# A third tile of rows, and longer waits between the stages of a chunk's tail

## Chip, cores and metric

The kernel runs on one core of one Trainium2 chip. The metric is device microseconds of one execution; times given for the kernel are medians over several runs.

## What is computed

One layer of graph attention on x (8 frames, 2048 rows, 256 channels) with a 2048 x 2048 adjacency mask, all in float32. Cut to what matters:

```python
qkv = x @ w_qkv                                   # 8 heads of 32 channels
scores = q @ k.T / sqrt(32), masked to -1e9 where adj == 0
t = softmax(scores) @ v
y = layernorm(x + t) * g1 + be1
f = relu(y @ w1 + b1) @ w2 + b2
z = layernorm(y + f) * g2 + be2
out = layernorm(x + z)
```

## The kernel before

**Main loop.** The 1024 items of `fast_path` are (frame f, chunk qc of 512 query rows, head group g of four heads, block mb of 128 keys): 8 x 4 x 2 x 16. An item is one step t of the loop at L599. In it, TensorE makes the scores of item t + 2 (`scores`, L222 to L234) in pairs of PSUM banks; VectorE adds the mask to them and writes an SBUF tile `p` of 128 x 2048 (L233, two instructions); ScalarE takes the exponential of item t + 1 in place (L237); TensorE multiplies item t's `p` with the values (L249) into the group's bank. The pool `pp` has 12 tiles. A chunk is two groups of 16 steps, so 32 steps.

**Sums of p.** The softmax denominators are column sums of all 16 `p` tiles. `add_up` folds them into few: blocks 3, 6, 8, 11, 13, 15 are added to block 0 by POOL (L271); two chains of three are added into blocks 1 and 2 by accumulating DMAs that POOL issues (L268); block 14 stays alone. `denominator` then multiplies the four tiles that remain with ones (L315), the last of them, block 0, not before `advance` has reached the step `ready`, which is the group's last step plus `SUM`. The sum is copied out of PSUM into `dT` (L317), transposed (L95) and inverted (L326).

**Side work.** Everything else is written as Python generators in the list `fill`: x transposes (`turn`), projections (`project`, `ask`), denominators, and, for each chunk, `outcome` (divides the attention result, adds x by an accumulating DMA, L339) and `tail`. `advance(t)` runs at the head of each step and resumes those that are ready, sorted by a due step. A number that a generator yields is a wait of so many steps; BANK asks for a PSUM bank, one new one per step; MORE asks to go on with the bank; WAIT holds it; ROOM waits until fewer than the allowed number of tails is open; TURNED waits for the tiles of the feed-forward part. Each step has credit for about one piece of matmul work, and for more only when something is due. All this is fixed when the program is built: on the chip each engine runs its instructions in that order and waits on semaphores.

**Tail of a chunk.** `tail` works on a tile `y` from the pool `yp` (two tiles): `norm` (statistics on VectorE, L278 and L279; 1 / sigma and the bias `nb` on POOL, L283 to L287; scale and shift on ScalarE, L290), `feed_forward` (transposes, rows g1r and be1b2r on POOL at L459 and L461, first products with `w1s`, second with `w2s`, sum at L483), `norm`, rows g2r and be2r on POOL (L363, L365), x added by DMA (L367), `norm`, and the store (L370). `per` is how many of the four row blocks are done in one step. In the last frame the chunk before the last uses `per` 2; the last chunk goes through `finish`, in two halves.

**Masks.** The mask of a chunk is 8 tiles of fp8, each for two blocks; they are made once, kept in DRAM, and loaded by SP for each later chunk (L151), into a pool `mkp` of 9 tiles. SP also issues the x and xT loads, the xT stores and the output.

Of the kernel before, what the change touches and what calls it, by code (L numbers as in the profile page):

```python
# [19 lines left out]
P = 128  # L20
# [41 lines left out]
def fast_path(ctx, tc, cst, x, adj, out, RS):  # L62
# [6 lines left out]
    mkp = ctx.enter_context(tc.tile_pool(name="mkp", bufs=MB // 2 + 1))  # L69
# [6 lines left out]
    yp = ctx.enter_context(tc.tile_pool(name="yp", bufs=2))  # L76
# [185 lines left out]
    SUM = 4  # L262
# [11 lines left out]
    def norm(t, per=1):  # L274
        mv = small.tile([P, TPC, nc.vector.BN_AGGR_DIM], F32, name="mv")
        for j in range(TPC):
            st = small.tile([P, nc.vector.BN_STATS_DIM], F32, name="st")
            nc.vector.bn_stats(st, t[:, j, :])  # L278
            nc.vector.bn_aggr(mv[:, j, :], st)  # L279
            if j % per == per - 1:  # L280
                yield 1
        rs = small.tile([P, TPC], F32, name="rs")
        nc.gpsimd.tensor_scalar(rs, mv[:, :, 1], EPS, 1.0, op0=ALU.add, op1=ALU.mult)  # L283
        nc.gpsimd.tensor_tensor(rs, rs, cst["mhalf"], ALU.pow)  # L284
        nb = small.tile([P, TPC], F32, name="nb")
        nc.gpsimd.tensor_tensor(nb, mv[:, :, 0], rs, ALU.mult)
        nc.gpsimd.tensor_scalar(nb, nb, -1.0, 1.0, op0=ALU.mult, op1=ALU.mult)  # L287
        yield 2
        for j in range(TPC):
            nc.scalar.activation(t[:, j, :], t[:, j, :], AF.Identity, bias=nb[:, j:j + 1], scale=rs[:, j:j + 1])  # L290
            if j % per == per - 1:
                yield 1
# [4 lines left out]
    def denominator(f, qc, g, ready):  # L297
# [7 lines left out]
        ps = bank()  # L305
        for n, block in enumerate(blocks):
# [4 lines left out]
            term = PT.pop((f, qc, g, block))  # L311
            state["credit"] -= 4 * CH
# [3 lines left out]
        dT = op.tile([P, CH], F32, name="dT")  # L316
# [16 lines left out]
    def outcome(f, qc):  # L333
# [7 lines left out]
        if (f, qc) == (F - 1, NCK - 2):  # L341
            start(begin + 5, tail(f, qc, y, xin, 2), begin + 8)
        else:
            start(begin + 10, tail(f, qc, y, xin), begin + 26)
# [12 lines left out]
    def tail(f, qc, y, xin, per=1):  # L357
# [10 lines left out]
        yield 7  # L368
# [68 lines left out]
    def finish(f, qc):  # L437
# [6 lines left out]
        while both:  # L444
            for e in list(both):
                if next(e, both) is both:
                    both.remove(e)

    def feed_forward(y):
# [22 lines left out]
        yield 1  # L472
# [31 lines left out]
    def advance(t, finish=False):  # L504
# [15 lines left out]
        for e in list(fill):  # L520
            while e[2] is not None and e[0] <= t and e is not state["holder"]:
# [8 lines left out]
                elif e[2] == TURNED and state["turned"] or e[2] == ROOM and state["tails"] == 2:  # L530
# [6 lines left out]
    LEAD = 2  # L537
# [61 lines left out]
    for t, (f, qc, g, mb) in enumerate(items):  # L599
        if g == 1 and mb % 2 and (f + 1 < F or qc + 1 < NCK):  # L600
            load_mask(f + (qc + 1) // NCK, (qc + 1) % NCK, mb // 2)
# [269 lines left out]
```

## Time and profile before

| what | value |
|---|---|
| median of 3 runs | 3241.72 us (3237.86 to 3245.61) |
| the profiled execution, own time | 3246.02 us |
| its span, first to last instruction | 3244.1 us |
| mean granted TensorE clock | 0.985 |
| TensorE matmuls busy | 3109.4 us, 96% |
| VectorE, ScalarE, POOL busy | 84%, 75%, 80% |
| L233 mask additions on VectorE | 2409.3 us, mean 1218 ns |
| L237 exponentials on ScalarE | 1956.1 us, mean 1910 ns |
| L271 sums on POOL | 1825.5 us, mean 4793 ns |
| mask loads by SP | 248, 128 KB each |

The profile is of one execution. A wait is put down to what ended it. "Busy" of TensorE is modelled from the instructions' sizes; engines wait in order, so an engine's idle time costs only where the work that ends last stands behind it. Times in the timeline count from the start of the span.

### The profile page before, as it was taken

To read this page: it belongs to the slowest core of one execution; us is meant where nothing else is said; L and a number is where in the kernel's file an instruction comes from. 1 tells how busy PE (TensorE), PEld (TensorE's weight loads), DVE (VectorE), ACT (ScalarE), POOL (GpSimd) and SP (SyncE) were. 2 spreads that over 40 slices of the span, in tenths; PEclk is the share of its full clock that TensorE was granted. 3 is DMA by queue.
4 is the path that set the end of the run, shared out by engine and by line. 5 is a ranking of instruction groups with operands and counts; after the bars stand their busy time and mean duration, and the time that the engine had idled before them with its cause. 6 is when DMAs were issued, how large, how long until landed. Compare 5 with 4: busy or idle time off the path is not lost.

```text
span 3244.1 us, 68406 instructions
## 1 busy us (share of the span) xinstructions
PE 3109.4 (96%) x28996; PEld 979.0 (30%) x28996; DVE 2735.7 (84%) x3203; ACT 2435.8 (75%) x1941; POOL 2592.2 (80%) x1358
## 2 busy tenths in 40 slices
PE   7899999999999999999999999999999999998985
PEld 4222333223332233322233323323233323332222
DVE  4888888888888888888988888888888888888975
ACT  3667778777777777778777778777778777777774
POOL 0568888888878888788887888888888788878884
PEclk8899999999999999999999999999999999999998
DMA  9688779778879788788787879878788878877763
GB/s 320 145 181 185 183 176 199 178 177 196 181 176 207 171 188 193 159 195 200 178 181 174 185 174 221 177 167 198 173 192 197 177 168 198 181 171 161 166 145 86
DMA packets 153240, 590.52 MB, mean 182 GB/s; under 512 B 15040, under 2 KB 67776, under 8 KB 103904
## 3 DMA queue, kind: packets, MB, share of 16 engines
q0 software_dynamic: 64416, 434.80, 66.9%
q1 hardware_dynamic: 87696, 149.98, 13.1%
q8 instruction: 229, 3.75, 0.4%
q10 hardware_dynamic: 816, 1.31, 0.1%
q14 instruction: 83, 0.68, 0.1%
HBM read 146.67 MB, written 37.75 MB: 57 GB/s over the span
## 4 chain that ended last, share of the span: by engine, by line
PE 75%; DVE 7%; POOL 5%; issue 4%; DMA 4%; ACT 2%; DVEq 0%; POOLq 0%; ACTq 0%
PE s L230 27%; PE x L249 24%; PE x L54 14%; PE x L315 6%; DVE p L233 6%; PE x L95 4%; DMA p<-p 3%; POOL p L271 2%; ACT p L237 1%; DMA mask<-md 1%; POOL y L365 1%; DVE st L278 1%; POOL y L363 0%; POOL y L461 0%; POOL y L459 0%
## 5 line engine op out<-in xcount | busy, mean ns | idle before, releaser
L233 DVE TENSOR_TENSOR p<-s,mask 128x1024 f32<-128x1024 f32 x2048 | 2409.3, 1218 | 372.7 <-PE s L230 209.9
L237 ACT ACTIVATE p<-p 128x2048 f32<-128x2048 f32 x1024 | 1956.1, 1910 | 521.4 <-DVE p L233 465.6
L271 POOL TENSOR_TENSOR p<-p 128x2048 f32<-128x2048 f32 x381 | 1825.5, 4793 | 223.7 <-ACT p L237 221.3
L230 PE MATMUL s<-qT,kT 32*128 32x512 f32 x8192 | 1173.8, 643 | 40.8 <-DVE p L233 35.9
L249 PE MATMUL x<-p,v 128*32 128x512 f32 x8192 | 1096.0, 607 | 16.7 <-ACT p L237 16.4
L268 POOL DMA_DIRECT2D p<-p x383 | 359.3, 956 | 306.9 <-ACT p L237 88.3
L230 PEld LDWEIGHTS s<-qT,kT 32*128 32x128 f32 x8192 | 321.1, 183 | 644.7 <-DVE p L233 587.2
L249 PEld LDWEIGHTS x<-p,v 128*32 128x32 f32 x8192 | 161.6, 108 | 797.8 <-issue 310.6
L315 PE MATMUL x<-p,ones 128*32 128x512 f32 x2080 | 268.2, 594 | 17.9 <-POOL p L271 11.1
L290 ACT ACTIVATE y<-y,nb,rs 128x256 f32<-128x256 f32 x372 | 218.7, 590 | 40.4 <-POOL nb L287 40.4
L54 PE MATMUL x<-in,wqkv 128*32 128x512 f32 x1888 | 243.5, 592 | 0.0
L278 DVE BATCH_NORM_STATS2 st<-y 128x6 f32<-128x256 f32 x372 | 154.9, 416 | 5.1 <-DMA y<-in_x_dram 5.1
L54 PE MATMUL x<-turned,w1s 128*32 128x512 f32 x992 | 123.5, 596 | 0.4 <-ACT in L166 0.4
L54 PE MATMUL x<-w2s,hT 128*32 128x256 f32 x2016 | 121.8, 382 | 2.1 <-DVE y L483 2.1
L54 PEld LDWEIGHTS x<-wqkv,in 128*32 128x32 f32 x3584 | 102.2, 110 | 63.4 <-issue 58.9
L315 PEld LDWEIGHTS x<-p,ones 128*32 128x32 f32 x2080 | 66.3, 110 | 178.2 <-issue 140.4
L54 PE MATMUL x<-wqkv,in 128*32 128x128 f32 x3584 | 117.3, 273 | 0.0
L54 PEld LDWEIGHTS x<-in,wqkv 128*32 128x32 f32 x1888 | 61.7, 110 | 140.9 <-issue 113.7
L284 POOL TENSOR_TENSOR rs<-rs,mhalf 128x4 f32<-128x4 f32 x93 | 96.3, 1036 | 7.8
L54 PEld LDWEIGHTS x<-w2s,hT 128*32 128x32 f32 x2016 | 65.4, 111 | 75.0 <-issue 33.0
L363 POOL TENSOR_TENSOR y<-y,g2r 128x1024 f32<-128x1024 f32 x31 | 82.5, 2663 | 5.3 <-ACT y L290 5.3
L461 POOL TENSOR_TENSOR y<-y,be1b2r 128x1024 f32<-128x1024 f32 x31 | 83.0, 2679 | 0.6
(116 smaller groups left out, 1335.7 us busy)
## 6 DMA issues: line engine op xcount, KB each, us to landing
p<-p POOLq DMA_DIRECT2D x383, 1024.0 KB, 10.4
in<-xd SPq DMA_DIRECT2D x87, 512.0 KB, 10.6
mask<-md SPq DMA_DIRECT2D x248, 128.0 KB, 7.9
y<-in_x_dram POOLq DMA_DIRECT2D x62, 512.0 KB, 8.1
p<-in_adj_dram SPq DMA_DIRECT2D x16, 1024.0 KB, 10.7
out_dram<-y SPq DMA_DIRECT2D x31, 512.0 KB, 6.2
in<-in_x_dram SPq DMA_DIRECT2D x29, 512.0 KB, 15.5
xd<-in SPq DMA_DIRECT2D x28, 512.0 KB, 11.2
```

The source lines that it names most:

```text
L54: nc.tensor.matmul(out[r:r + D], lhsT[:, r:r + D], rhs, start=start, stop=stop)
L95: nc.tensor.transpose(ps[:, j * P:(j + 1) * P], s, ident)
L230: nc.tensor.matmul(ps2[half][:, j, :], KT[f, mb // TPC, g][r:r + D, (mb % TPC) * P:(mb % TPC + 1) * P], QT[f, qc, g][r:r + D, :], start=Tr ...
L233: nc.vector.tensor_tensor(pt[:, 2 * half:2 * half + 2, :], ps, MK[f, qc, mb // 2][:, mb % 2, None, :].to_broadcast([P, 2, CH]), ALU.add)
L237: nc.scalar.activation(PT[item], PT[item], AF.Exp, scale=1.0 / math.sqrt(D))
L249: nc.tensor.matmul(O[grp][r:r + D, :], V[f, mb // TPC, g][:, mb % TPC, r:r + D], PT[item][:, h, :], start=(mb == 0), stop=(mb == LAST))
L268: nc.gpsimd.dma_start(PT[f, qc, g, chain[0]], PT.pop(item), accum_op=ALU.add)
L271: nc.gpsimd.tensor_tensor(first, first, PT.pop(item), ALU.add)
L278: nc.vector.bn_stats(st, t[:, j, :])
L284: nc.gpsimd.tensor_tensor(rs, rs, cst["mhalf"], ALU.pow)
L290: nc.scalar.activation(t[:, j, :], t[:, j, :], AF.Identity, bias=nb[:, j:j + 1], scale=rs[:, j:j + 1])
L315: nc.tensor.matmul(ps[r:r + D, :], cst["ones"], term[:, h, :], start=(n == 0), stop=(n == len(blocks) - 1))
```

## The change

The pool of row tiles `yp` goes from 2 to 3, and up to three tails may be open. The room for it comes from the mask pool (9 to 8 tiles) and from the tile `dT`, which is dropped: the copied denominators go into the first quarter of the first term's `p` tile. Mask loads are written six steps later in the program (`LATE`). `SUM` goes from 4 to 5. `norm` waits 4 steps (3 with `per` 2) and not 2 between POOL's part and ScalarE's; the second products wait 3 steps and not 1; the last norm waits 9 (7 with `per` 2) and not 7. Tails start 12 steps after their division and not 10, with a later due step; in the last frame all tails use `per` 2 and start 8 steps after it (before, only that of the chunk before the last, 5 steps after it). `finish` gives way for a step after each round of its two halves.

```diff
--- before.py
+++ after.py
@@ -66,14 +66,14 @@
 
     LD = 3
     dp = ctx.enter_context(tc.tile_pool(name="dp", bufs=1, space=bass.MemoryType.DRAM))
-    mkp = ctx.enter_context(tc.tile_pool(name="mkp", bufs=MB // 2 + 1))
+    mkp = ctx.enter_context(tc.tile_pool(name="mkp", bufs=MB // 2))
     ld = ctx.enter_context(tc.tile_pool(name="ld", bufs=LD))
     kp = ctx.enter_context(tc.tile_pool(name="kp", bufs=3 * NCK - 1))
     qp = ctx.enter_context(tc.tile_pool(name="qp", bufs=4))
     vp = ctx.enter_context(tc.tile_pool(name="vp", bufs=3 * NCK - 1))
     pp = ctx.enter_context(tc.tile_pool(name="pp", bufs=12))
     work = ctx.enter_context(tc.tile_pool(name="work", bufs=1))
-    yp = ctx.enter_context(tc.tile_pool(name="yp", bufs=2))
+    yp = ctx.enter_context(tc.tile_pool(name="yp", bufs=3))
     op = ctx.enter_context(tc.tile_pool(name="op", bufs=1))
     small = ctx.enter_context(tc.tile_pool(name="small", bufs=4))
 
@@ -259,7 +259,7 @@
     ALONE = 14
 
     ENDED = MB - 5
-    SUM = 4
+    SUM = 5
 
     def add_up(item):
         f, qc, g, mb = item
@@ -285,7 +285,7 @@
         nb = small.tile([P, TPC], F32, name="nb")
         nc.gpsimd.tensor_tensor(nb, mv[:, :, 0], rs, ALU.mult)
         nc.gpsimd.tensor_scalar(nb, nb, -1.0, 1.0, op0=ALU.mult, op1=ALU.mult)
-        yield 2
+        yield max(5 - per, 2)
         for j in range(TPC):
             nc.scalar.activation(t[:, j, :], t[:, j, :], AF.Identity, bias=nb[:, j:j + 1], scale=rs[:, j:j + 1])
             if j % per == per - 1:
@@ -303,17 +303,19 @@
             late = {n: len(items) - k for n, k in ((2, 2), (3, 1), (4, 1), (5, 0), (6, 0), (7, 0))}
         yield BANK
         ps = bank()
+        spare = None
         for n, block in enumerate(blocks):
             if n:
                 yield MORE
             while state["now"] < late.get(n, 0):
                 yield WAIT
             term = PT.pop((f, qc, g, block))
+            spare = spare or term
             state["credit"] -= 4 * CH
             for h in range(4):
                 r = D * h
                 nc.tensor.matmul(ps[r:r + D, :], cst["ones"], term[:, h, :], start=(n == 0), stop=(n == len(blocks) - 1))
-        dT = op.tile([P, CH], F32, name="dT")
+        dT = spare[:, 0, :]
         nc.scalar.copy(dT, ps)
         yield 1
         yield BANK
@@ -338,10 +340,10 @@
         yield from divide(f, qc, y)
         nc.gpsimd.dma_start(y, xin, accum_op=ALU.add)
         begin = items.index((f, qc, 1, LAST)) + SUM + 2
-        if (f, qc) == (F - 1, NCK - 2):
-            start(begin + 5, tail(f, qc, y, xin, 2), begin + 8)
+        if f == F - 1:
+            start(begin + 8, tail(f, qc, y, xin, 2), begin + 12)
         else:
-            start(begin + 10, tail(f, qc, y, xin), begin + 26)
+            start(begin + 12, tail(f, qc, y, xin), begin + 30)
 
     def divide(f, qc, y):
         rc = RC.pop((f, qc))
@@ -365,7 +367,7 @@
         nc.gpsimd.tensor_tensor(z, z, rows(cst["be2r"]), ALU.add)
         yield 1
         nc.gpsimd.dma_start(z, xin, accum_op=ALU.add)
-        yield 7
+        yield 11 - 2 * per
         yield from norm(z, per)
         nc.sync.dma_start(out[f, qc * CH:(qc + 1) * CH, :].rearrange("(p j) c -> p j c", p=P), z)
         state["tails"] -= 1
@@ -445,6 +447,7 @@
             for e in list(both):
                 if next(e, both) is both:
                     both.remove(e)
+            yield 1
 
     def feed_forward(y):
         yield TURNED
@@ -469,7 +472,7 @@
                 columns(ps, w1s[:, a, d * P:(d + 1) * P], yT[:, a, :], start=(a == 0), stop=(a == 1))
             nc.scalar.activation(hT[:, d, :], ps, AF.Relu, bias=cst["b1s"][:, d:d + 1], scale=1.0)
         state["turned"] = False
-        yield 1
+        yield 3
         z = y
         for jj in range(0, TPC, 2):
             yield BANK
@@ -527,14 +530,14 @@
                     inputs = inputs and not any(u is not None for u in live[:INPUTS - e[2]])
                     if not inputs:
                         break
-                elif e[2] == TURNED and state["turned"] or e[2] == ROOM and state["tails"] == 2:
+                elif e[2] == TURNED and state["turned"] or e[2] == ROOM and state["tails"] == 3:
                     break
                 resume(e, t)
             while e is state["holder"] and more():
                 resume(e, t)
 
     items = [(f, qc, g, mb) for f in range(F) for qc in range(NCK) for g in range(2) for mb in range(MB)]
-    LEAD = 2
+    LEAD, LATE = 2, 6
     FRAME = 2 * NCK * MB
 
 
@@ -597,8 +600,9 @@
         pass
     state["side"] = 0
     for t, (f, qc, g, mb) in enumerate(items):
-        if g == 1 and mb % 2 and (f + 1 < F or qc + 1 < NCK):
-            load_mask(f + (qc + 1) // NCK, (qc + 1) % NCK, mb // 2)
+        uf, uqc, ug, umb = items[max(t - LATE, 0)]
+        if ug == 1 and umb % 2 and (uf + 1 < F or uqc + 1 < NCK):
+            load_mask(uf + (uqc + 1) // NCK, (uqc + 1) % NCK, umb // 2)
         for what, *which in NEXT.get(t % FRAME, []):
             to = f if what is ask and which[0] else f + 1
             if to < F:
```

## The prediction

> **What bounds the kernel now.** I read the page's busy shares first, then PE's own waits, then the timeline around one of its gaps.
>
> ```profile
> PE 3109.4 (96%) x28996; PEld 979.0 (30%) x28996; DVE 2735.7 (84%) x3203; ACT 2435.8 (75%) x1941; POOL 2592.2 (80%) x1358
> ```
>
> PE is the bound, but its busy time is modelled, so I checked it by steps. In the timeline the gap from the first L249 matmul of one step to that of the next depends only on the side work ("fill") between them. I call eight L54 or L315 matmuls (32 small ones for V or the second products), or four transposes, a unit. Medians: one unit 2.92 us, two 3.78, transposes of dT or oT 2.75, of y 2.65, nothing 2.56 (2.49 at best). A unit is thus 3.78 - 2.92 = 0.86, a step without fill would need 2.06, and an **empty step** wastes about 0.45: there DVE's two L233 adds (2.36) set the pace. A steady frame of 128 steps holds 144 units, 18 of them second in their step, and 2 empty steps (144 - 18 + 2 = 128).
>
> What a step takes beyond its kind's median is a stall. Frames 1 to 6: 41.0 us in all. Frame 7: 20.9. Frame 0: 8.6. The waits of PE name the releasers:
>
> ```profile
> PE s L230 <- DVE p L233: 35.9, 64, 6.5
> PE x L249 <- ACT p L237: 16.4, 10, 5.1
> ...
> PE x L315 <- POOL p L271: 11.1, 6, 2.1
> ...
> PE x L315 <- DMA p<-p: 6.9, 5, 3.9
> ```
>
> Columns: total us, times, longest. The third is a denominator term waiting for POOL's sums, the second a value product waiting for the exponential. Why the exponential is late shows in the timeline of frame 3, group 3 (groups of 16 steps, numbered from 0), step 14:
>
> ```profile
> 1427.85 4.88 POOL L271 TENSOR_TENSOR p<-p 128x2048 f32<-128x2048 f32 x1
> ...
> 1434.50 0.19 POOL L287 TENSOR_SCALAR nb<-nb 128x4 f32<-128x4 f32 x1
> ...
> 1434.73 0.60 ACT L290 ACTIVATE y<-y,nb,rs 128x256 f32<-128x256 f32 x1 [4.05 <-POOL nb L287]
> ...
> 1435.23 1.89 ACT L237 ACTIVATE p<-p 128x2048 f32<-128x2048 f32 x1
> ...
> 1437.18 0.64 PE L249 MATMUL x<-p,v 128*32 128x512 f32 x4 [2.19 <-ACT p L237]
> ```
>
> The norm's small POOL operations queue behind a 4.88 us addition; ACT reaches the norm two steps after they were issued, sits 4.05 us, the exponential behind it starts late, and PE idles 2.19 us. The same spot costs in every frame from 1 on.
>
> **What the Trainium skill says.** "Perfetto Trace Analysis", section Per-engine timelines, says that ACT, DVE and GPSIMD take work strictly first in, first out: the three lines from nb to L237 agree. The same page, section Optimization Strategy, advises finding the saturated engine's gaps and what releases them; repeating gaps may mean missing buffers. Here the repeated gap is a late POOL result; no row shows DVE waiting for a y buffer. "GPSIMD Engine Reference", section Elementwise — side-by-side cycle accounting, gives 4497 ns for a 2048-element fp32 addition; L271's mean here is 4793, so POOL spends 1.6 steps on each of six such sums per 16 steps, and lag of two steps is easy.
>
> **The change part by part.** Steps r count from the first step after a 512-row chunk ends; a chunk has 32.
>
> *Norms wait 4 steps instead of 2 (3 with two rows at a time).* No instruction is added. Two steps are 5.8 us, more than the 4.05. Group 3 steps 14 and 15, frames 1 to 6: 1.42, 1.69, 2.26, 1.91, 0.90, 1.97, 1.70 = 11.9; group 7 step 11: 1.20 and 0.35. Of 13.4 I take 12 off. In frame 7 the same stall is 5.13 + 1.40; only one step is gained, but the older tail also runs at other steps: 4.5 off, of 6.5. Between zero and all is the bound.
>
> *SUM 4 to 5.* The fourth term was held to `advance` 19 after its group began and would be held to 20. I looked at where it falls: counting the fill after step s as s, it comes at 3 or later in 62 of 63 groups (19 times at 3, which is `advance` 20), once at 2. So the hold itself binds once, at most one empty step, 0.45: I take zero. Its other effect is that division starts at 6 and not 5, behind dT at the same place: zero, at most one step.
>
> *Tail start +2, product wait 1 to 3, last norm 2 later.* These move POOL's four 2.6 us row operations. Before, L363 and L365 fall between step 12 of even groups and step 1 of odd ones, where additions 13 and 15 of the sum chain also queue. In frame 3 they ran at 1484.32 and 1491.16, addition 15 from 1494.75 to 1499.63, and the fourth term waited: group 5 steps 2 to 4 cost 2.56, 3.86, 1.59, 3.86, 1.81, 3.60 = 17.3, group 7 step 3 another 0.8. After, by hand: norm 18 to 29, y transposed at 30 and 31, first products 33 to 36, denominators next, second products about 39 to 41, norm to 53, L363 at 54 and 55, step 6 or 7 of odd groups, far from the closing sums. L459 and L461 come at 0 or 1 of even groups, behind addition 15, as they already do in group 2 without a stall. I take 11 of 18.1, because third terms also wait for the DMA sums, whose issues share POOL; bound 0 to 18. The second products' own wait (group 6 step 0, on L461 through L483) is 0.73 + 1.14 + 0.41 + 0.65 = 2.9: two more steps, all off.
>
> *Last frame.* All three tails now start at +8. The third-last DVE stop is the clearest gain:
>
> ```profile
> 3118.78 0.87 POOL L339 DMA_DIRECT2D y<-in_x_dram  x1 [1.47 <-DVE y L353]
> ...
> 3128.36 0.43 DVE L278 BATCH_NORM_STATS2 st<-y 128x6 f32<-128x256 f32 x1 [5.13 <-DMA y<-in_x_dram]
> ...
> 3130.80 2.09 PE L230 MATMUL s<-qT,kT 32*128 32x512 f32 x8 [6.52 <-DVE p L233]
> ```
>
> The statistics are issued two steps after the transfer, which takes 9.5 us; DVE's mask additions queue behind. Steps 10 and 11 of group 6 lose 7.10 + 1.22. With three to four more steps the transfer has landed: 8 off. At the end, the last chunk no longer runs as one block; the second-last tail's L363 and L365 (2.40 each) stand on POOL ahead of the finish's first norm, about 3 us late, while its four statistics (2.3) go between the finish's and not behind: +2 net, -3 to +5.
>
> *Longer tails, third y tile.* A tail lasts from step 6 to about 77 where it was 5 to some 66 (counted from the code's yields and the steps above); two per 64 steps no longer suffice, the third removes a wait of the next chunk at ROOM. Covered: 0; without it each chunk would slip some ten steps.
>
> *dT in the first term's tile.* No copy is added; L317 writes another place. The tile stays until the transposes, 3 to 7 steps longer. Unfinished p tiles peak at 10 of 12 when a group begins (4 old heads, 3 new, 3 in the pipeline), and the kept tile is one of the four: 0, at worst a DVE wait of under a step (2 us) per group.
>
> *Masks: 8 tiles, loaded 6 steps later.* The 248 loads and SP's issue cost stay. Before, a mask landed 41 us (median; least 20.7) before the L233 that reads it, and took 10.1 us to land (longest 23.4). One tile fewer frees it two steps later, -6; on SP it now queues behind six more steps of x and xT transfers and out stores, each of which may wait for ACT. If SP keeps step exactly it is issued 6.5 steps, 19 us, ahead. Mostly covered; 1 us for a few late ones, 20 at the bound. The x and xT loads no longer stand behind masks that wait for their tile: nothing PE shows, 0.
>
> *Fill.* The product phase leaves the end of odd groups. There steps 9 to 15 may lack units, though projections move up. I allow 2 more empty steps per frame, 7 x 2 x 0.45 = 6; bounds -6 (the present 2 go) and +20.
>
> **Sum.** 12 + 4.5 + 11 + 2.9 + 8 = 38.4 off; 2 + 1 + 6 on, and 2 for POOL lag meeting a wait elsewhere: -27. The profiled execution took 3246.0 (span 3244.1 and 1.9 around it), 4.3 above the median; it becomes 3219, the median 3241.7 - 27 = **3215**.
>
> **Rivals.**
> - *POOL's lag only moves.* POOL is 80% busy either way; the denominators' 17.3 stay and the norms' stall reappears at other steps: only 2.9 + 8 + 6 off against 11 on: about 3236. For it: the hold of SUM doesn't bind. Against: group 2 has this phase now, and no stall.
> - *SUM alone does nothing and the rest works:* that is inside my sum already, the group 5 loss then stays wholly: 3226.
> - *Slower: empty steps.* Each tail moves five units out of odd groups. If projections can't fill them (an xT needs a free `in` tile), 31 chunks x 5 x 0.45 = 70 us come on against 38: 3241.7 + 32 = 3274. It decides from 38 / 31 / 0.45 = 2.7 more empty steps per chunk. Against it: 14 units of projections and x transposes per chunk have only about 12 free steps, so backlog should fill them; group 1 shows such backlog as double steps.
>
> **How the numbers follow.** Main course 0.57, SUM rival 0.13, lag moves 0.15, slower 0.15 (empty steps, with late masks in it). About 0.2%, 6.5 us, is what a measurement here tells from no change. The first two lie below 3235; of the third 0.02 does, and 0.13 lies within: faster 0.72, same 0.13, slower 0.15. Range: all stalls gone and no new empty step gives 3195; the top takes in the milder slower cases, 3252.
>
> **What would show it.** Right: L290 waits for nb fall from 40.4 us to under 10; the 6.52 us gap is gone; L363 runs in steps 5 to 8 of odd groups; L315 waits for POOL are halved; 2 to 5 empty steps per frame. Wrong: over 8 empty steps per frame, DVE waits on mask loads, or L315's waits at a new step.

## The result, and the profile after

The kernel after takes **3381.99 us** (median of 4 runs, 3377.37 to 3382.84) against 3242.98 (median of 4) for the kernel before: a ratio of 1.0428, 95% interval 1.041 to 1.0446. It is 139 us slower; the forecast was 27 us faster, with a range that ended at 3252. The profiled execution is the run of 3377.37, its span 3375.5 us: 131.4 more than before.

Busy times, from the page's first part:

```profile
PE 3143.5 (93%) x28996; PEld 982.2 (29%) x28996; DVE 2736.5 (81%) x3203; ACT 2440.3 (72%) x1941; POOL 2590.3 (77%) x1358
```

No engine has more to do: the instruction counts are those of before, and DVE and POOL are busy within 2 us of before. PE's modelled busy time is 34 us up, its share down from 96 to 93%. So the 131 us are waits. The granted clock is no rival: it was 0.985 before and 0.980 after, and the median of a step with one unit is 2.92 us in both. The waits of the kernel after (total us, times, longest), DVE's lines first, then PE's:

```profile
DVE p L233 <- PE s L230: 209.3, 333, 6.0
DVE p L233 <- DMA p<-p: 164.7, 67, 6.3
```

```profile
PE s L230 <- DVE p L233: 147.5, 180, 3.9
...
PE x L317 <- DMA p<-p: 6.0, 3, 3.4
...
PE x L249 <- ACT p L237: 2.8, 5, 1.3
```

The same DVE line of the kernel before:

```profile
DVE p L233 <- DMA p<-p: 1.7, 1, 1.7
```

The line to see is the second. DVE's mask addition L233 writes a fresh `p` tile, and that tile was last read by a sum made by DMA. Before, it waited for such a sum once, for 1.7 us; now 67 times, 164.7 us. PE then waits for DVE's scores (35.9 us before, 147.5 now). PE's waits for a term from POOL (11.1 before) are gone from the list, and those for the exponential fell from 16.4 to 2.8: what the forecast aimed at did go. (Lines move by two or three: L315, L353, L363, L365, L459 and L461 of before are L317, L355, L365, L367, L462 and L464 after.)

The step method of the prediction says where. Each entry is the time that steps took beyond the median that their kind has in the kernel before, an empty step with the 0.5 us or so that it wastes; "even" and "odd" are groups of 16 steps, numbered from 0 in a frame, with step numbers within the group:

| kernel | even 0-3 | even 4-10 | even 11-15 | odd 0-6 | odd 7-13 | odd 14-15 | frames 0 and 7 | all | span |
|---|---|---|---|---|---|---|---|---|---|
| before | 3.3 | 3.9 | 6.3 | 19.3 | 3.8 | 12.0 | 49.4 | 98.0 | 3244.1 |
| after | 22.8 | 68.4 | 28.7 | 0.6 | 28.4 | 0.2 | 79.8 | 228.7 | 3375.5 |

The first six columns are frames 1 to 6. The totals differ by 130.7, the spans by 131.4: the table holds the whole loss. The old stalls (odd 0-6, odd 14-15) are gone, and four new ones stand elsewhere.

**Where it comes from.** The largest, even 4 to 10, in frame 3, group 4. POOL before, from just ahead of the group (which starts at 1440.96):

```profile
1437.58 2.69 POOL L461 TENSOR_TENSOR y<-y,be1b2r 128x1024 f32<-128x1024 f32 x1
1439.92 14.10 POOL L271 TENSOR_TENSOR p<-p 128x2048 f32<-128x2048 f32 x3
1453.93 0.88 POOL L268 DMA_DIRECT2D p<-p  x1
```

And after (the group starts at 1499.57, its step 7 at 1521.98):

```profile
1499.81 9.52 POOL L271 TENSOR_TENSOR p<-p 128x2048 f32<-128x2048 f32 x2
1509.28 2.38 POOL L462 TENSOR_TENSOR y<-y,g1r 128x1024 f32<-128x1024 f32 x1
1511.75 2.38 POOL L464 TENSOR_TENSOR y<-y,be1b2r 128x1024 f32<-128x1024 f32 x1
1514.08 4.59 POOL L271 TENSOR_TENSOR p<-p 128x2048 f32<-128x2048 f32 x1
1518.58 0.88 POOL L268 DMA_DIRECT2D p<-p  x1
```

Before, the row operation was over when the group began: three sums, then the DMA that adds block 4 (L268), 13.0 us into the group. Now L462 and L464 stand between the second and the third of those sums, and the DMA is issued 19.0 us into it. From its issue to its landing it takes 7.0 us (median), and until then block 4's tile is not free. Here is DVE, which needs that tile for the scores of step 7:

```profile
1518.70 2.36 DVE L233 TENSOR_TENSOR p<-s,mask 128x1024 f32<-128x1024 f32 x2 [0.86 <-POOL p L271]
1526.23 2.35 DVE L233 TENSOR_TENSOR p<-s,mask 128x1024 f32<-128x1024 f32 x2 [5.18 <-DMA p<-p]
...
1532.05 2.35 DVE L233 TENSOR_TENSOR p<-s,mask 128x1024 f32<-128x1024 f32 x2 [2.87 <-DMA p<-p]
```

The transfer lands at 1526.11, DVE goes on at 1526.23, and steps 7 and 8 are 3.1 and 1.8 us too long. The second wait, at 1532.05, ends with the sum of block 5, the next that POOL issued. Followed landing by landing, DVE's 164.7 us are 82.9 for block 4, 53.9 for block 5, and 27.3 for blocks 10 and 12 of the group before.

The late sum also meets fewer free tiles. In this group four steps of first products now go ahead of the denominators. Before, the four remaining `p` tiles of the ended group were let go one by one at steps 2 to 5; now three go at steps 5 and 6, and the one that lends its first quarter to `dT` at step 9, with the transposes. With so few free tiles, DVE meets the one that a transfer still reads. How much a late sum would cost with the tiles let go early, no run shows by itself. "Perfetto Trace Analysis", section Optimization Strategy, says that the same gap repeating on the engine that should be saturated can mean too little memory for the next tile. In the kernel before no line showed that; in this one the 67 waits do. "DMA: Bandwidth & Descriptors", section Anatomy of one DMA — SWDGE (gpsimd) path, puts any semaphore wait of a transfer on the issuing engine; the tail experiments below show that on POOL.

The stall at even 0-3 is the same wait, with the last sums of the odd group before it. POOL in frame 5, group 3, and then DVE in step 1 of group 4:

```profile
2290.71 2.37 POOL L367 TENSOR_TENSOR y<-y,be2r 128x1024 f32<-128x1024 f32 x1
2293.02 0.91 POOL L268 DMA_DIRECT2D p<-p  x1
```

```profile
2317.46 2.36 DVE L233 TENSOR_TENSOR p<-s,mask 128x1024 f32<-128x1024 f32 x2 [2.30 <-DMA p<-p]
```

L365 and L367 now start at steps 5 and 8 of odd groups, and L367 stands ahead of the DMA of block 7, which goes out at step 8.96 (median) where it was 7.64. Block 10 follows it in the same chain and lands 3.6 us after the even group has begun, where it was 0.7 us ahead of it. In these steps of frames 1 to 6 DVE waits 23.0 us for the sums of blocks 10 and 12.

The even 11-15 stall is of another kind, in frame 3, group 4 again:

```profile
1540.24 0.42 DVE L278 BATCH_NORM_STATS2 st<-y 128x6 f32<-128x256 f32 x1
1540.70 0.18 DVE L279 BATCH_NORM_AGGREGATE mv<-st 128x2 f32<-128x6 f32 x1
1540.80 0.66 DVE L355 TENSOR_TENSOR y<-x,rc 128x512 f32<-128x512 f32 x1
1541.37 2.35 DVE L233 TENSOR_TENSOR p<-s,mask 128x1024 f32<-128x1024 f32 x2
```

The second norm's statistics and the next chunk's division L355 fall in the same two steps. DVE needs from 1540.24 to 1543.63, 3.39 us, in steps that PE's transposes would end in 2.75, and nothing on DVE waits.

### The profile page after: what moved, and what is told of

Its sections match the earlier page's. It is cut to its first block, busy times and chain, and to the rows that moved or that the text cites. A ratio compares the mean times of both kernels' runs of the same rounds, so it can differ in the third digit from the quotient of the medians.

```text
span 3375.5 us, 68264 instructions
## 1 busy us (share of the span) xinstructions
PE 3143.5 (93%) x28996; PEld 982.2 (29%) x28996; DVE 2736.5 (81%) x3203; ACT 2440.3 (72%) x1941; POOL 2590.3 (77%) x1358
## 5 line engine op out<-in xcount | busy, mean ns | idle before, releaser
L233 DVE TENSOR_TENSOR p<-s,mask 128x1024 f32<-128x1024 f32 x2048 | 2411.6, 1219 | 536.7 <-PE s L230 209.3
L230 PE MATMUL s<-qT,kT 32*128 32x512 f32 x8192 | 1180.5, 646 | 152.3 <-DVE p L233 147.5
L268 POOL DMA_DIRECT2D p<-p x383 | 384.2, 1008 | 321.5 <-ACT y L290 96.3
L317 PE MATMUL x<-p,ones 128*32 128x512 f32 x2080 | 266.8, 596 | 6.0 <-DMA p<-p 6.0
L317 PEld LDWEIGHTS x<-p,ones 128*32 128x32 f32 x2080 | 67.7, 111 | 164.2 <-issue 146.8
L365 POOL TENSOR_TENSOR y<-y,g2r 128x1024 f32<-128x1024 f32 x31 | 78.2, 2523 | 11.4 <-ACT y L290 11.4
L319 ACT COPY p<-x 128x512 f32<-128x512 f32 x64 | 37.4, 585 | 56.8 <-PE x L317 56.7
## 6 DMA issues: line engine op xcount, KB each, us to landing
xd<-in SPq DMA_DIRECT2D x28, 512.0 KB, 10.5
```

The costliest lines, as they stand in the source:

```text
L230: nc.tensor.matmul(ps2[half][:, j, :], KT[f, mb // TPC, g][r:r + D, (mb % TPC) * P:(mb % TPC + 1) * P], QT[f, qc, g][r:r + D, :], start=Tr ...
L233: nc.vector.tensor_tensor(pt[:, 2 * half:2 * half + 2, :], ps, MK[f, qc, mb // 2][:, mb % 2, None, :].to_broadcast([P, 2, CH]), ALU.add)
L268: nc.gpsimd.dma_start(PT[f, qc, g, chain[0]], PT.pop(item), accum_op=ALU.add)
L317: nc.tensor.matmul(ps[r:r + D, :], cst["ones"], term[:, h, :], start=(n == 0), stop=(n == len(blocks) - 1))
L365: nc.gpsimd.tensor_tensor(z, z, rows(cst["g2r"]), ALU.mult)
```

## The experiments

Theory **T** (tiles): the loss is that `p` tiles come back late, because POOL's row operations delay the DMA sums and the old tiles are held longer. Rivals: **K**, the kept tile of `dT` alone; **S**, `SUM` alone; **C**, DVE is crowded by the moved norms; **M**, masks and the `y` tile. Each run was compared with the kernel before on the same chip (medians there 3241.81 to 3242.82). The same table for these runs:

| kernel | even 0-3 | even 4-10 | even 11-15 | odd 0-6 | odd 7-13 | odd 14-15 | frames 0 and 7 | all |
|---|---|---|---|---|---|---|---|---|
| b_keep | 2.8 | 3.5 | 6.3 | 24.6 | 7.0 | 10.5 | 51.7 | 106.3 |
| b_pp11 | 3.7 | 3.1 | 7.0 | 42.1 | 2.4 | 8.8 | 56.0 | 123.1 |
| a_own_k10 | 25.3 | 42.5 | 29.2 | 0.6 | 13.1 | 0.1 | 76.8 | 187.6 |
| a_first | 79.7 | 0.5 | 0.5 | 1.9 | 14.4 | 0.2 | 67.9 | 165.0 |
| a_rows | 19.5 | 3.8 | 29.2 | 0.6 | 28.9 | 0.2 | 68.7 | 150.9 |
| a_apart | 4.7 | 31.3 | 1.7 | 0.6 | 32.0 | 0.2 | 61.0 | 131.5 |
| a_apart_own | 4.6 | 6.6 | 1.1 | 0.6 | 13.3 | 0.2 | 50.7 | 76.9 |
| a_best | 4.3 | 2.6 | 1.0 | 0.6 | 13.3 | 0.2 | 51.2 | 73.1 |
| b_sum5 | 0.4 | 1.8 | 4.0 | 48.7 | 50.9 | 18.4 | 54.1 | 178.3 |
| b_sum5_only | 3.5 | 1.4 | 31.1 | 27.1 | 9.6 | 9.4 | 47.6 | 129.6 |
| b_tail1 | 0.4 | 4.4 | 6.3 | 43.8 | 33.5 | 24.4 | 57.8 | 170.6 |
| a_mem | 0.4 | 1.6 | 3.8 | 47.3 | 38.8 | 24.0 | 58.9 | 174.7 |
| a_sum4 | 26.9 | 79.0 | 15.8 | 0.6 | 7.7 | 0.2 | 79.1 | 209.3 |
| b_norm3 | 19.4 | 3.6 | 6.3 | 41.4 | 1.2 | 0.2 | 50.3 | 122.5 |
| b_masks | 0.4 | 3.9 | 6.3 | 18.4 | 2.8 | 9.6 | 46.7 | 88.0 |
| b_last | 3.7 | 3.9 | 6.3 | 20.0 | 3.2 | 10.0 | 51.9 | 99.1 |

### Does the kept tile cost, and do tiles run short?

**b_keep**: the kernel before, with `dT` in the first term's tile.

```diff
+        spare = None
...
+            spare = spare or term
...
-        dT = op.tile([P, CH], F32, name="dT")
+        dT = spare[:, 0, :]
```

> The kernel before, with one part of the change alone: the copied denominators go into the first term's p tile, which is so kept until their transposes; order and waits are those of before. Theory 'kept tile' (the p pool lacks a tile because of dT): VectorE waits for DMAs that still read p appear here too, 50 to 110 us, so about 3300 to 3350. Theory 'late denominators' (the pool runs short because the first products now stand ahead of the denominators in even groups): here the denominators are as early as before, so at most 10 us of such waits, 3240 to 3255. Theory 'both needed': 3255 to 3275.

Measured: 3253.98, ratio 1.0042 (1.0026 to 1.0057), 11 us. DVE's waits for the DMA sums are 14.0 us in 9 waits, where there were 1.7 in one. Small, and not nothing.

**a_own_k10**: the kernel after, with a tile of its own for `dT`; one key tile fewer makes room.

```diff
-    kp = ctx.enter_context(tc.tile_pool(name="kp", bufs=3 * NCK - 1))
+    kp = ctx.enter_context(tc.tile_pool(name="kp", bufs=3 * NCK - 2))
...
-        dT = spare[:, 0, :]
+        dT = op.tile([P, CH], F32, name="dT")
```

> The changed kernel, with dT back in a tile of its own (one key tile of 11 is given up for its room); order of all work as after the change. 'Kept tile': the waits of VectorE for p (170 us after) go, about 3270. 'Late denominators': three of the four heads are still held to steps 5 to 7, most waits stay, 3345 to 3375. 'Both needed': half goes, 3310. A loss from the tenth key tile would show as ScalarE copies of kT that wait.

Measured: 3326.88, ratio 1.0262 (1.0245 to 1.0279): 55 us of the 139 back. That is five times what b_keep adds to the kernel before; I read it as the price of a tile where more of them are held already. Of the columns it is even 4-10 (68.4 to 42.5) and odd 7-13 (28.4 to 13.1) that fall. The tenth key tile takes little: ScalarE's copies into key tiles wait 8.5 us more, for PE's scores. DVE's waits, in the chain of waits:

```profile
DVE p L233 <- DMA p<-p: 113.0, 54, 6.3
```

K as the sole cause falls: most of the waits remain with no tile kept.

**b_pp11**: the kernel before, with one `p` tile fewer. The order on every engine is the same as before, so only the reuse of tiles differs.

```diff
-    pp = ctx.enter_context(tc.tile_pool(name="pp", bufs=12))
+    pp = ctx.enter_context(tc.tile_pool(name="pp", bufs=11))
```

> The kernel before with 11 p tiles and not 12, nothing else: the order on every engine stays. If before had a tile to spare in the p pool, as the prediction had it (10 of 12): 3240 to 3250. If a free tile is not a usable one, because the DMA or POOL's sum that reads it last is still under way: waits of VectorE for DMAs into p as after the change, 3290 to 3400.

Measured: 3269.77, ratio 1.0085 (1.0068 to 1.0102), 28 us. The same line of its chain of waits:

```profile
DVE p L233 <- DMA p<-p: 51.0, 35, 3.4
```

This settles the point on tiles: taking a single one away brings the kind of wait that the kernel after shows, though most of it at other places (odd 0-6 goes from 19.3 to 42.1) and with less loss than the 3290 expected. The 12 tiles had no spare.

### What holds the tiles, and what makes the sums late?

**a_first**: the kernel after, with the denominators due `SUM` steps sooner, and so ahead of the first products.

```diff
-            start(t + 2, denominator(f, qc, g, t + SUM), t + SUM + 4)
+            start(t + 2, denominator(f, qc, g, t + SUM), t + 4)
```

> The changed kernel, with the denominators due at step t + 4 and not t + SUM + 4, so that they stand ahead of the tail's first products in even groups, and the division ahead of the second products; dT stays in the kept tile. 'Kept tile': no gain, 3360 to 3385. 'Late denominators' with 'division and second norm meet': both losses go, 3230 to 3265, and waits of VectorE for DMAs into p fall from 165 us to under 30.

Measured: 3311.16, ratio 1.0213 (1.0195 to 1.0231), 71 us back. The stall at even 4-10 is gone (68.4 to 0.5), as T asks. Even 11-15 goes too (28.7 to 0.5), as C asks: the division now comes ahead of the second products and so doesn't meet the second norm. But even 0-3 now costs 79.7, so the 3230 to 3265 expected were missed. The DMA of block 4 also goes out earlier here, at step 3.95 of even groups and not 5.43, so this run doesn't tell the held tiles from the late sum. Its PE waits:

```profile
PE s L230 <- DVE p L233: 65.2, 114, 2.3
PE x L317 <- DMA p<-p: 53.5, 34, 3.5
```

The second line is new: 34 times a denominator term waits on PE for its DMA sum, where the kernel after has 3 such waits. The tiles can't be let go sooner than POOL and the DMAs finish them. The first products ahead of the denominators hide that delay on PE and pay for it in tiles.

**a_rows**: the kernel after, with L462 and L464 moved behind the first products.

```diff
-        yield 1
-        nc.gpsimd.tensor_tensor(y, y, rows(cst["g1r"]), ALU.mult)
-        yield 1
-        nc.gpsimd.tensor_tensor(y, y, rows(cst["be1b2r"]), ALU.add)
+        yield 2
...
-        yield 3
+        yield 1
+        nc.gpsimd.tensor_tensor(y, y, rows(cst["g1r"]), ALU.mult)
+        yield 1
+        nc.gpsimd.tensor_tensor(y, y, rows(cst["be1b2r"]), ALU.add)
+        yield 1
```

> The changed kernel, with POOL's two row operations of the feed-forward part issued behind the first products (two of the three steps of the new wait) and not ahead of them, so that on POOL they no longer stand between the closing sum of a group (block 15) and the next group's block 3 and the DMA of block 4. Theory 'rows ahead of the DMA of block 4': that DMA is issued some two steps earlier, VectorE's waits for it at steps 7 and 8 of even groups (120 us of 165) fall to under 40, and the time to about 3320. Theory 'only the number of p tiles counts': waits and time as after, 3370 to 3385.

Measured: 3311.6, ratio 1.0219 (1.0201 to 1.0238), 70 us back. (Its profile is of an execution of 3299.7.) The issue of the DMA of block 4 comes at step 4.12 of even groups (median) where the kernel after has 5.43, and the stall at even 4-10 goes from 68.4 to 3.8 while no other column of frames 1 to 6 moves by more than 3.3. DVE's waits:

```profile
DVE p L233 <- DMA p<-p: 58.3, 41, 3.7
```

In frame 3, group 4, the denominators stand in the same steps as in the kernel after and the tile is kept as long; only the sum is earlier, and steps 7 and 8 lose nothing. The two row operations in that place are thus worth 65 us. What remains is at even 0-3 and 11-15 and in odd groups.

**a_apart**: the kernel after, with the second norm four steps later.

```diff
-        yield 1
+        yield 5
```

(It is the wait in `tail` between `feed_forward` and the second `norm`.)

> The changed kernel, with 4 steps more between the second products and the second norm, so that its statistics no longer fall into the steps of the division. Theory 'division and second norm meet': steps 11 and 12 of even groups fall from 3.39 to about 2.75, in frames 1 to 6 28 us less, in all some 33 us, 3345 to 3352. If that coincidence is harmless: 3375 to 3390. The waits of VectorE for p should stay near 165 us in either case.

Measured: 3273.81, ratio 1.0093 (1.0072 to 1.0114): 108 us back. The crowding's own column goes from 28.7 to 1.7, as C has it. But even 0-3 (22.8 to 4.7) and half of even 4-10 went too, so the gain is far more than C's; that was a miss. The second norm's small POOL operations and the two row operations L365 and L367 behind them move by the same four steps; the DMA of block 4 is issued at step 4.56 and not 5.43 of even groups. Even 0-3 goes with them: the DMA of block 7 now goes out ahead of the two rows, at step 7.37 of odd groups and not 8.96, and block 10 lands 2.8 us ahead of the even group and not 3.6 us into it. DVE's waits:

```profile
DVE p L233 <- DMA p<-p: 93.7, 45, 4.0
```

**a_apart_own**: both, the later norm and a `dT` of its own.

```diff
-    kp = ctx.enter_context(tc.tile_pool(name="kp", bufs=3 * NCK - 1))
+    kp = ctx.enter_context(tc.tile_pool(name="kp", bufs=3 * NCK - 2))
...
-        dT = spare[:, 0, :]
+        dT = op.tile([P, CH], F32, name="dT")
...
-        yield 1
+        yield 5
```

> The changed kernel with both mends, four steps more ahead of the second norm and a dT tile of its own (ten key tiles). Adding the gains: after 3382, less 108 for the first, less 55 for the second: 3219, and less than before if they add. If both mend the same waits: about 3265.

Measured: 3226.6, ratio 0.9953 (0.9935 to 0.9971). Two small edits turn 139 us slower into 15 us faster. The gains are 55 and 108 apart and 155 together: here they nearly add.

### How much is SUM, and how?

**b_sum5**: the kernel before, with `SUM` 5 alone.

```diff
-    SUM = 4
+    SUM = 5
```

> The kernel before with SUM 5 alone: denominators due one step later, division and tail one step later. The prediction priced this at zero: then 3240 to 3250. Theory 'one step moves the whole tail against POOL's sums' (the memory side of the change, which holds SUM 5, lost 79 us, the kept tile alone 11): 3280 to 3310, with new stalls in odd groups at steps 2, 3, 7 to 9 and 14.

Measured: 3326.89, ratio 1.0266 (1.0251 to 1.0282), 85 us: the largest surprise. The constant does three things: it holds the fourth term, it sets the step at which a denominator falls due (`t + SUM + 4`), and through `begin` it starts divisions and tails. The next two runs take the third apart from the first two.

**b_sum5_only**: the hold and the due step alone, `begin` as it was.

```diff
-    SUM = 4
+    SUM = 5
...
-            begin = items.index((f, qc, g, LAST)) + SUM + 2
+            begin = items.index((f, qc, g, LAST)) + 6
...
-        begin = items.index((f, qc, 1, LAST)) + SUM + 2
+        begin = items.index((f, qc, 1, LAST)) + 6
```

> The kernel before with SUM 5 for the denominators' hold and due step alone; division and tail start where they did (begin = last step + 6). If the denominators' step is what costs 85 us: about 3325. If the tail's step is: 3240 to 3255.

Measured: 3278.96, ratio 1.0114 (1.0097 to 1.0131), 36 us. The hold itself binds in one group of 63 (the fourth term goes from step 2 to 3). The due step does more: in 13 groups (groups 1 and 2 of their frames) the fourth term was made at the end of step 6 because it was due, and now comes at step 7. In group 2 transposes and division go with it. POOL and then DVE in frame 2, from the timeline:

```profile
991.23 1.84 POOL L268 DMA_DIRECT2D p<-p  x2 [0.28 <-issue]
994.62 0.87 POOL L339 DMA_DIRECT2D y<-in_x_dram  x1 [1.54 <-DVE y L353]
```

```profile
1009.30 0.43 DVE L278 BATCH_NORM_STATS2 st<-y 128x6 f32<-128x256 f32 x1 [4.38 <-DMA y<-in_x_dram]
```

The transfer of x goes out behind the later division, and the statistics, whose step did not move, meet it in flight: 4.38 us here, 2.2 to 4.5 in group 2 of every frame from 1 on (27 us in all).

**b_tail1**: `SUM` 4 as before, divisions and tails one step later.

```diff
-            begin = items.index((f, qc, g, LAST)) + SUM + 2
+            begin = items.index((f, qc, g, LAST)) + 7
...
-        begin = items.index((f, qc, 1, LAST)) + SUM + 2
+        begin = items.index((f, qc, 1, LAST)) + 7
```

> The kernel before with division and tail one step later (begin = last step + 7), the denominators as before. If the tail's step against POOL's sums is what costs 85 us: 3310 to 3330, with late DMAs of block 4 in odd groups and waits of VectorE for p at steps 7 and 8. If the denominators' step is: 3240 to 3255.

Measured: 3317.77, ratio 1.0218 (1.0197 to 1.024): a shift of one step costs 75 us, most of `SUM`'s 85. POOL in frame 3, group 1, from the timeline:

```profile
1333.43 1.83 POOL L268 DMA_DIRECT2D p<-p  x2 [0.28 <-issue]
1334.64 5.22 POOL L271 TENSOR_TENSOR p<-p 128x2048 f32<-128x2048 f32 x1
1341.21 0.88 POOL L268 DMA_DIRECT2D p<-p  x1 [1.35 <-DMA p<-p]
1341.83 4.87 POOL L271 TENSOR_TENSOR p<-p 128x2048 f32<-128x2048 f32 x1
1348.01 0.87 POOL L268 DMA_DIRECT2D p<-p  x1 [1.31 <-DMA p<-p]
```

and DVE in the same stretch:

```profile
1340.80 2.36 DVE L233 TENSOR_TENSOR p<-s,mask 128x1024 f32<-128x1024 f32 x2 [2.60 <-DMA p<-p]
...
1347.57 2.36 DVE L233 TENSOR_TENSOR p<-s,mask 128x1024 f32<-128x1024 f32 x2 [3.62 <-DMA p<-p]
```

In groups 1 and 7 the row operation L365 of the tail now runs after the start of the group (at 1318.25 here, the group starting at 1317.49) and so ahead of its first sums, and the DMA of block 4 goes out at step 5.62 of odd groups (median) and not at 4.85. The next DMA of the same chain adds into the same tile; POOL itself stands at its issue until the earlier one has landed, with all later sums behind it. These waits of POOL are 75.5 us before and 108.4 here. In group 1 DVE then waits for tiles (37.7 us in frames 1 to 6, for blocks 4 and 5), though the fourth term comes at step 6 as before. In group 7 it is PE that waits, 15.1 us at steps 2 and 3, for a denominator term whose sum ends with block 12; and the norms' stall at odd 14-15 doubles. The lag passes from POOL to the DMA and back to POOL. By themselves this run and b_sum5_only cost 75 and 36 us, and `SUM`, which does both, 85.

**a_sum4**: the kernel after, with `SUM` 4.

```diff
-    SUM = 5
+    SUM = 4
```

> The changed kernel with SUM back at 4, all else as after. If SUM's step costs the same here as in the kernel before (85 us): about 3297. If the longer waits set the place of the tail here anyway, so that SUM only moves the stalls: 3350 to 3400.

Measured: 3362.09, ratio 1.0367 (1.0346 to 1.0388): only 20 us back of the 85. In the kernel after the rows fall at other steps; I take it that a shift by one has another price for that reason, but no run shows it. S falls as the sole cause, and so does any sum of the parts' single costs.

### The waits, the memory, the masks, the last frame

**a_mem**: the kernel after, with the starts and waits of the tail, the last frame's too, as before; it keeps three `y` tiles, 8 mask tiles with `LATE`, the kept tile, `SUM` 5 and the step between the rounds of `finish`.

```diff
-        yield max(5 - per, 2)
+        yield 2
...
-        if f == F - 1:
-            start(begin + 8, tail(f, qc, y, xin, 2), begin + 12)
+        if (f, qc) == (F - 1, NCK - 2):
+            start(begin + 5, tail(f, qc, y, xin, 2), begin + 8)
...
-            start(begin + 12, tail(f, qc, y, xin), begin + 30)
+            start(begin + 10, tail(f, qc, y, xin), begin + 26)
...
-        yield 11 - 2 * per
+        yield 7
...
-        yield 3
+        yield 1
```

> The changed kernel's memory alone: three y tiles, eight mask tiles loaded six steps later, the kept p tile, SUM 5 and the finish in rounds; all waits and starts of the tail as before. If the loss comes from the tail's waits and starts: as with the kept tile alone, 3245 to 3262. If the later masks or SUM matter: over 3270.

Measured: 3320.66, ratio 1.0243 (1.0206 to 1.028). Its stalls stand where b_sum5 has them, in odd groups, and its time is that of b_sum5 less 6 us, which is within its interval. So the memory part adds nothing that shows beside `SUM`, and the longer waits move the loss from odd groups to even ones and, with the last frame's edits, add 61 us to it.

**b_norm3**: the kernel before, with the wait inside `norm` one step longer, and the last norm's wait two shorter.

```diff
-        yield 2
+        yield 3
...
-        yield 7
+        yield 5
```

> The kernel before, with one part of the change alone, in half its size: the norm waits 3 steps and not 2, and the last norm 5 and not 7, so that the tail keeps its length. If the norm's wait was worth what the prediction took off: the stall at step 14 of odd groups (10 us in frames 1 to 6, 5 in frame 7) goes for the most part, 3228 to 3236. If POOL's lag or the order that goes with it undoes it: 3240 or more.

Measured: 3267.39, ratio 1.0068 (1.0044 to 1.0091), 26 us slower. The stall at odd 14-15 goes from 12.0 to 0.2: the norms' part of the theory holds, and a single step is enough. But DVE gets two other waits:

```profile
DVE y L483 <- POOL y L461: 40.1, 16, 4.2
...
DVE st L278 <- DMA y<-in_x_dram: 36.2, 21, 5.9
```

The first was 9.5 us: everything behind the norm came later on POOL, with the second products where they were. The second is the last norm meeting its transfer, because this run took two steps from that wait.

**b_masks**: the kernel before, with 8 mask tiles, loaded six steps later.

```diff
-    mkp = ctx.enter_context(tc.tile_pool(name="mkp", bufs=MB // 2 + 1))
+    mkp = ctx.enter_context(tc.tile_pool(name="mkp", bufs=MB // 2))
...
-    LEAD = 2
+    LEAD, LATE = 2, 6
...
-        if g == 1 and mb % 2 and (f + 1 < F or qc + 1 < NCK):
-            load_mask(f + (qc + 1) // NCK, (qc + 1) % NCK, mb // 2)
+        uf, uqc, ug, umb = items[max(t - LATE, 0)]
+        if ug == 1 and umb % 2 and (uf + 1 < F or uqc + 1 < NCK):
+            load_mask(uf + (uqc + 1) // NCK, (uqc + 1) % NCK, umb // 2)
```

> The kernel before with eight mask tiles, loaded six steps later. Theory 'masks are covered': 3238 to 3248, and no wait of VectorE for a mask. If the later masks are what cost the 68 us between the kept tile alone and the whole memory side: about 3300.

Measured: 3234.81, ratio 0.998 (0.9973 to 0.9987), 7 us faster; I have no cause for the 7. M falls. In the kernel after a mask still lands 34.0 us (median; least 12.6) before its L233.

**b_last**: the kernel before, with the last frame's edits.

```diff
-        if (f, qc) == (F - 1, NCK - 2):
-            start(begin + 5, tail(f, qc, y, xin, 2), begin + 8)
+        if f == F - 1:
+            start(begin + 8, tail(f, qc, y, xin, 2), begin + 12)
...
+            yield 1
```

> The kernel before with the last frame's edits alone: all three tails start 8 steps after the division with two row blocks per step, and the finish gives way between its rounds. The prediction took 8 us off for the statistics that no longer wait for x and put 2 on at the end: 3236. If denser statistics on VectorE eat the gain: 3242 or more.

Measured: 3246.37, ratio 1.0011 (1.0002 to 1.0019), 4 us slower. The stop of 6.52 us is gone, as forecast. But `per` 2 puts two row blocks' statistics in one step. DVE and PE in the last frame:

```profile
3141.91 0.42 DVE L278 BATCH_NORM_STATS2 st<-y 128x6 f32<-128x256 f32 x1
3142.36 0.18 DVE L279 BATCH_NORM_AGGREGATE mv<-st 128x2 f32<-128x6 f32 x1
3142.46 0.40 DVE L278 BATCH_NORM_STATS2 st<-y 128x6 f32<-128x256 f32 x1
3142.89 0.18 DVE L279 BATCH_NORM_AGGREGATE mv<-st 128x2 f32<-128x6 f32 x1
3143.00 2.36 DVE L233 TENSOR_TENSOR p<-s,mask 128x1024 f32<-128x1024 f32 x2
```

```profile
3144.28 1.14 PE L230 MATMUL s<-qT,kT 32*128 32x512 f32 x8 [1.22 <-DVE p L233]
```

In an empty step DVE is the pace; 1.09 us of statistics ahead of L233 makes that step 1.2 us longer, and now two more tails do so.

### A version that beats both

**a_best**: the kernel after, with a_apart, a `dT` of its own and the rows behind the first products.

```diff
-    kp = ctx.enter_context(tc.tile_pool(name="kp", bufs=3 * NCK - 1))
+    kp = ctx.enter_context(tc.tile_pool(name="kp", bufs=3 * NCK - 2))
...
-        dT = spare[:, 0, :]
+        dT = op.tile([P, CH], F32, name="dT")
...
-        yield 1
+        yield 5
...
-        yield 1
-        nc.gpsimd.tensor_tensor(y, y, rows(cst["g1r"]), ALU.mult)
-        yield 1
-        nc.gpsimd.tensor_tensor(y, y, rows(cst["be1b2r"]), ALU.add)
+        yield 2
...
-        yield 3
+        yield 1
+        nc.gpsimd.tensor_tensor(y, y, rows(cst["g1r"]), ALU.mult)
+        yield 1
+        nc.gpsimd.tensor_tensor(y, y, rows(cst["be1b2r"]), ALU.add)
+        yield 1
```

> The changed kernel with three mends: second norm four steps later, dT in a tile of its own (ten key tiles), and the row operations of the feed-forward part behind the first products. If the row operations still hold up the DMA of block 4: waits of VectorE for DMAs into p fall from 43 us to under 20, 3212 to 3222. If that DMA is already early enough, the same as without this mend, 3222 to 3230.

Measured: 3222.93, ratio 0.9942 (0.9929 to 0.9956), 19 us under before and 159 under after. From its chain of waits:

```profile
PE s L230 <- DVE p L233: 43.8, 80, 4.1
...
DVE p L233 <- DMA p<-p: 16.7, 15, 3.3
```

DVE's 164.7 us are down to 16.7, and PE's 147.5 to 43.8. All this with the longer waits, the third `y` tile and `SUM` 5 in place. The DMA of block 4 goes out at step 3.87 in even groups. Beside a_apart_own (3226.6) the third mend shows no gain clear of noise: the intervals of the two ratios overlap. DVE's waits are under the 20 us expected, but the time fits the other case, "already early enough".

What the runs support is T, with C for some 27 us of it: the whole loss, and more, can be taken back by letting the sums run earlier, the tiles go and the norm out of the division's steps.

## Why the prediction was wrong

All five signs that the prediction named for being right came true, and those for being wrong showed next to nothing (one wait of DVE for a mask, 0.4 us, and 6.0 us of PE for terms of a sum): they watched the stalls that it priced, and not the new place of the work. By its own terms. Right in cause and near in size:

- *Norms, -12:* odd 14-15 went from 12.0 to 0.2. ACT's waits for `nb` fell from 40.4 us to 5.0, in the groups of the two kernels:

```profile
L290 ACT ACTIVATE y<-y,nb,rs 128x256 f32<-128x256 f32 x372 | 218.7, 590 | 40.4 <-POOL nb L287 40.4
L290 ACT ACTIVATE y<-y,nb,rs 128x256 f32<-128x256 f32 x372 | 217.5, 591 | 5.0 <-POOL nb L287 5.0
```

- *Denominators, -11 of 18.1:* odd 0-6 went from 19.3 to 0.6, all of it. L365 and L367 start at steps 5 and 8 of odd groups, around the 6 or 7 forecast. *Second products, -2.9:* DVE's wait for L461 is off the list.
- *Last frame, -8, and end +2:* the stop at group 6 (7.54 and 1.66 of excess) is gone, and from the last step's start to the end is 49.3 us where it was 47.6. What the term left out is `per` 2 in two more tails: in frame 7 of the kernel after, steps 14 and 15 of groups 3 to 6 are empty steps with two or four row blocks' statistics ahead of L233, and cost 15.6 us (8.7 before, 6.6 of it the norms' stall). In the kernel before, the edit by itself comes out at +4.
- *Fill, +6, and with it the slower rival:* frames 1 to 6 have 2 empty steps each, before and after. The prediction's empty steps were not the way to slower.
- *Masks, +1:* -7 in the kernel before. (The reading of 10.1 us to land, 23.4 at most, was off: the trace has a median of 7.9 and 24.8 at most. Nothing hung on it.)

Wrong:

- **"L459 and L461 come at 0 or 1 of even groups, behind addition 15, as they already do in group 2 without a stall."** The order was about right, though on POOL they start at steps 2.4 to 3.8 in three groups of four: they stand behind sum 15 and ahead of sum 3. The step that failed is the next one: I asked only whether the *closing* sums were free of them, and not what was queued behind them on POOL. It was sum 3 and the DMA of block 4, and behind that DMA a `p` tile. a_rows prices it: 65 us of stall, 70 us of time. For L363 and L365 of before I made the same slip: "far from the closing sums" was right, but they came ahead of the DMA of block 7, and even 0-3 lost 19.5 us.
- **"Unfinished p tiles peak at 10 of 12 when a group begins", with 0 for the kept one.** I counted a tile as free when its last PE reader was behind it. Tiles in a sum are read by POOL or by a DMA until this lands; b_pp11 shows that not one of 12 was spare. The kept tile cost 11 us in the kernel before and 55 in the one after.
- **"So the hold itself binds once, at most one empty step, 0.45: I take zero."** The hold does bind once. But `SUM` is also in the step at which denominators fall due, and this I left out: it delays group 2's division, and the two cost 36 us. The division's new start I took as "at most one step". A step of shift of the tails costs 75 us in the kernel before. Neither adds to the rest: taken out of the kernel after, `SUM` gives back 20.
- **Crowding on DVE.** No term of mine had it. L355 and the second norm's statistics now share steps: 27 us, which a_apart takes away.
- **"2 for POOL lag meeting a wait elsewhere."** This is the term that holds the first two errors, and it was too small by a factor of some fifty (even 0-3, even 4-10 and odd 7-13 hold 119.6 us after, 11.0 before; of odd 7-13 some 10 us stay in a_best too, and are no lag). In the rival "POOL's lag only moves" I let the lag reappear at the old price. The new place had another price, because `p` tiles and not just one ACT wait hung on it.

What stays open: the third `y` tile was not run by itself; of the 30 us that frames 0 and 7 lose only the last frame's empty steps were looked at; a late sum was not run apart from held tiles; and the single costs on the kernel before do not add up to the kernel after's, so no share of the 139 us is given to each edit.

## What to carry to other kernels

When a fixed order is shifted, ask for each moved instruction what stands *behind* it on its engine and which buffer that holds: a few microseconds on POOL ahead of a DMA that frees a tile cost more here than all the stalls that the shift removed. Count a pool's tiles to the landing of the last reader, transfers included, and try the pool with one fewer: if that costs, there is no slack to lend. And let the signs of being wrong include waits that don't exist yet: here every sign of being right came true. Losses of such shifts need not add (`SUM`: 85 us alone, 20 out of the bundle), so a bundle of them is best tried one by one and then in pairs.

## What the runs showed of the hardware that I had not expected

An accumulating transfer on a tile that an earlier one still adds into holds up POOL at its issue (108.4 us in 51 waits in b_tail1; 75.5 in 32 before, the longest 5.5), and not just the transfer: sums that need nothing of it stand behind. And a kernel whose engines are 75 to 96% busy can lose 2.2% (b_tail1) to a single step of shift, some 3 us in 3242, with not one instruction added.
